# Buffers and due times of the weighed edge scores in a two-layer graph kernel: six for four, and eight held chunks for nine

## The chip, the cores and the metric

The kernel runs on one core of one Trainium2 chip. The metric is the device time of one execution in microseconds (us); lower is better. A profiled execution is one run with the hardware profiler on; its times are told from the start of its span.

## What is computed

The inputs are `x`, 16 batches of 1024 nodes with 256 features, one sparse 1024 x 1024 matrix `adj` that is used in both layers, and small weights, all in float32. The first layer is an attention over `adj`; the second scores every edge and sends messages along it. Cut to what matters:

```
# layer 0, for each batch
feats = x @ W1.T;  f1 = feats @ W2 + b2
h = softmax(leaky_relu(f1[:, None] + f1[None, :]) + adj) @ feats + bias2 + x
# layer 1, for each batch
hidden[u, v] = relu(h[u] @ W1u + h[v] @ W1v + b1)
S[u, v] = sigmoid(hidden[u, v] @ W2 + b2)
a[v] = sum_u S[u, v] * adj[u, v] * h[u]
m[v] = (sum_u adj[u, v] * h[u]) * h[v]
out = beta1 * h + beta2 * (a @ Wa + ba) + beta3 * (m @ Wm + bm)
```

S counts only where `adj` isn't zero, so it is worked out for listed edges alone.

## The kernel before, in words

**Groups and chunks.** The 16 batches are taken in three groups of 5, 5 and 6 (`GROUPS`; 0, 1 and 2 here). Nodes are cut into 8 chunks of 128. For each group the core writes the two ends of the edge scores (`pu_d`, `pw_d`), h times Wa (`ha_d`) and the rest of the output (`zb_d`) to HBM, scores the edges, and at last sums over edges.

**Scores.** The edge list has 135 slots of 128 edges each (`SLOTS`). For a slot and all batches of a group POOL gathers a row of each edge's end (`fetch`, L1212 for the u side and L1219 for the v side; five buffers `gv`), DVE compares it with the other end (`compare`, L1248), ACT sums it, one instruction a batch (`sums`, L1262; every eighth slot of group 2 on DVE, L1259), and after each part of 4 to 16 slots ACT applies tanh (`gates`, L1270) and DVE adds one (L1289). POOL scatters the scores of each slot into the dense SA of the group in HBM (`scatter`, L1228). The scatters stand in a list `late`, out of which one or two are taken at each slot and all that are left at the end.

**The sum over edges.** The groups come in the order 1, 0, 2. For each group, each of the 8 column chunks `vc` and each of the 8 row chunks `c` there is one chunk of work, 192 in all and numbered here from 0 in this order: SP loads the 128 x 128 scores of all the group's batches (`load_sa`, L1332, tile `sat`, `SA` = 7 buffers); ACT copies them apart by batch (`part_sa`, L1345, tile `apart`, four buffers); DVE multiplies them by `adj` (`weigh_sa`, L1350, in place); PE multiplies them with h times Wa (`gather`, L1363, one matmul for each batch, which the trace shows as two instructions of 256 columns). After the eighth row chunk DVE adds the sum to the rest of the output (`finish_z`, L1386), ACT's queue stores it (`store_z`, L1390), and SP's queue loads the rest of a later column chunk (`load_zb`, L1373, two buffers).

**Held chunks of h times Wa.** PE's other operand, `ha_g`, is held for all 8 row chunks of a group, 640 KB each, in a ring of `HA` = 9 buffers (`load_ha`, L1318). There are 24 loads, numbered by group order and row chunk. A load can leave when the chunk `HA` places before it was read for the last time, in the eighth column chunk of its group. The sixth batch of group 2 lies in another tile, `rest`.

**What sets the order.** Nothing is left to a scheduler. Each step is put into a `Timetable` (L347) with a due time, and all are emitted in the order of due times; each engine and each DMA queue works in that order. PE's due times come from a running sum of matmul columns (a chunk of groups 0 and 1 is 5 x 256 columns, 2.13 us; one of group 2 2.56 us), the others are set relative to it. `begins[p]` is when PE is due to begin chunk p. Copies stand 8.2 us and weighings 6.0 us ahead of it (L1720, L1721). A load of SA stands 4.0 us ahead of the chunk 7 places before, whose buffer it takes (L1716). The slots of a group are evenly spaced between two set times; in group 2 from 1351.3 to 1872.0 in the table, so 3.86 us apart. The loads of `ha_g` beyond the first nine stand 2.4 us after the begin of the chunk that frees their buffer (L1711, L1712); the ninth stands in group 1's second column chunk (L1709). Between the halves of most column chunks PE also works off messages of batches that were put off (`follows`), with no chunk of the edge sum in them; there is none inside or behind the last column chunk of group 0, and a long one stands between groups 1 and 0.

The program says of the buffers and due times:

```python
    HA = 9
    SA = 7
...
        apart = st["apart", g, vc, c] = room(g).tile(
            [P, SIZE[g], P], F32, name="apart", bufs=4
        )
...
        due = when[0] - 36.0 + 4.0 * i if i < SA else begins[parts[i - SA]] - 4.0
...
        times.at(begins[p] - 8.2, lambda p=p: part_sa(*p))
        times.at(begins[p] - 6.0, lambda p=p: weigh_sa(*p))
```

Of the kernel before, what the change touches and what calls it, by code (L numbers as in the profile page):

```python
# [8 lines left out]
F32 = mybir.dt.float32  # L9
# [5 lines left out]
P = 128  # L15
# [356 lines left out]
def edge_layers(  # L372
# [40 lines left out]
    NG = len(GROUPS)  # L413
    SIZE = [hi - lo for lo, hi in GROUPS]
# [786 lines left out]

    PARTS = [16, 32, 48, 64, 80, 96, 112, 124, 131, len(SLOTS)]
    AHEAD = GV - 2
    HA = 9
    SA = 7
    late = []

# [105 lines left out]
    def room(g):  # L1313
        return pools["last" if g + 1 == NG else "late"]

    def load_ha(g, c):
        st["ha", g, c] = pools["late"].tile([P, CUT * D], F32, name="ha_g", bufs=HA)
        nc.sync.dma_start(  # L1318
            out=st["ha", g, c], in_=ha_d[g][c * P : (c + 1) * P, : CUT * D]
        )  # L1320
# [7 lines left out]
    def load_sa(g, vc, c):  # L1328

        n = SIZE[g]  # L1330
        sat = st["sat", g, vc, c] = room(g).tile([P, P, n], F32, name="sat", bufs=SA)
        nc.sync.dma_start(  # L1332
            out=sat.rearrange("p v g -> p (v g)"),
            in_=sa_d[g].rearrange("(c p v) g -> c p (v g)", p=P, v=N)[
                c, :, vc * P * n : (vc + 1) * P * n
            ],
        )

    def part_sa(g, vc, c):

        sat = st.pop(("sat", g, vc, c))
        apart = st["apart", g, vc, c] = room(g).tile(
            [P, SIZE[g], P], F32, name="apart", bufs=4
        )
        nc.scalar.copy(apart.rearrange("p g v -> p v g"), sat)  # L1345

    def weigh_sa(g, vc, c):
        apart = st["apart", g, vc, c]
        a = adj_sb[:, c, vc * P : (vc + 1) * P]
        nc.vector.tensor_tensor(  # L1350
            apart, apart, a.unsqueeze(1).to_broadcast([P, SIZE[g], P]), ALU.mult
        )
# [108 lines left out]
    times = Timetable()  # L1461
# [196 lines left out]
    when = []  # L1658
    begins = {}
# [17 lines left out]
    due = when[last] - 30.0  # L1677
# [27 lines left out]
    for n, (g, c) in enumerate((g, c) for g in order for c in range(C)):  # L1705
        if n < C:
            due = opened + 2.0 + (when[0] - 14.0 - opened) * n / C
        elif n < HA:
            due = when[2 + n - C] + 0.1  # L1709
        else:  # L1710
            k, c1 = divmod(n - HA, C)  # L1711
            due = begins[order[k], C - 1, c1] + 2.4  # L1712
        times.at(due, lambda g=g, c=c: load_ha(g, c))
    parts = list(begins)
    for i, p in enumerate(parts):
        due = when[0] - 36.0 + 4.0 * i if i < SA else begins[parts[i - SA]] - 4.0  # L1716
        if p[0] + 1 == NG:
            due = max(due, ended + 0.1 + 0.01 * i)
        times.at(due, lambda p=p: load_sa(*p))
        times.at(begins[p] - 8.2, lambda p=p: part_sa(*p))  # L1720
        times.at(begins[p] - 6.0, lambda p=p: weigh_sa(*p))  # L1721
    for i, (g, vc, half) in enumerate(halves):
        if half == 0:
            due = when[0] - 20.0 + 8.0 * i if i < 4 else when[i - 2] + 5.0
            if g + 1 == NG:
                due = max(due, ended + 0.2)
# [4 lines left out]
@with_exitstack  # L1731
def tile_graph_layers(ctx: ExitStack, tc: tile.TileContext, *args):
    nc = tc.nc
    I32 = mybir.dt.int32
    hold = ctx.enter_context(tc.tile_pool(name="hold", bufs=1))
    flag = hold.tile([1, 1], I32, name="flag")
    edge_layers(tc, *args, flag)
    over = nc.values_load(
        flag[0:1, 0:1],
        min_val=0,  # L1740
        max_val=1,
        skip_runtime_bounds_check_because="it is a comparison's result",
    )
    with tc.If(over > 0):
        dense_layers(tc, *args)
# [43 lines left out]
```

## Time and profile before

| what | us |
| --- | --- |
| three timed runs | 2081.66, 2082.96, 2084.30 (median 2082.96) |
| the profiled execution, own time | 2087.25 |
| its span | 2085.5 |
| PE busy in the span | 2023.7 |
| DVE, ACT, POOL busy | 1569.9, 1374.0, 1137.4 |
| first matmul of the edge sum, of group 0, of group 2 | 1419.6, 1680.8, 1910.6 |
| last matmul of the edge sum starts | 2078.2 |

The mean granted clock of TensorE is 0.997 of full speed. A row of the page's groups has the line, the engine, the operation and its tiles (output, arrow, inputs), how often it ran, its busy time and mean length, and behind the second bar the idle time of the engine just before it and who ended that. A row of the waits has who waited, for whom, the us in total, the times and the longest. In the timeline a row has its start, its length, engine, line and tiles; "SPq" and "ACTq" are the issue of a DMA by that queue, and a DMA lands later than its row ends. Tiles are named as in the program: `sat` is SA as loaded, `apart` SA copied apart and weighed, `ha_g` h times Wa, `gv` the gathered ends, `lg` the scores, `sa_d` SA in HBM, `pzg` and `pzh` the outputs of the edge sum.

### The profile page before, as it was taken

How to read it: one execution, taken by the hardware profiler on the slowest of the kernel's cores; microseconds unless marked ns; L12 is line 12 of the kernel's file. 1: busy time of each engine (PE TensorE's matmuls, PEld its weight loads, DVE VectorE, ACT ScalarE, POOL GpSimd, SP SyncE). 2: the span in 40 equal slices, each digit the busy share in tenths (PEclk: the TensorE clock that was granted, in tenths of full speed). 3: DMA queues.
4: the chain of work that ended last, by engine and by line, in shares of the span. 5: the costliest groups of instructions: out<-in, count | busy, mean ns of one | idle time of the engine just before them, and what ended most of it. 6: DMA issues, size and time to landing. Idle time of an engine off the chain costs nothing.

```text
span 2085.5 us, 28967 instructions
## 1 busy us (share of the span) xinstructions
PE 2023.7 (97%) x8577; PEld 1551.1 (74%) x8577; DVE 1569.9 (75%) x2348; ACT 1374.0 (66%) x4842; POOL 1137.4 (55%) x974
## 2 busy tenths in 40 slices
PE   8999999999999999999999999899999989999998
PEld 6888887777776868677888886457676666768887
DVE  7799884677877777677878886578888878885544
ACT  4211222577777767687888777577888878886654
POOL 1122221267676767678777777666767766773000
PEclk9999999999999999999999999999999999999999
DMA  6689776788888889789999989899999999997773
GB/s 219 244 310 347 286 294 244 255 262 285 286 279 270 282 283 293 262 293 297 318 300 323 328 302 312 317 396 414 382 392 366 412 415 397 387 402 265 282 234 123
DMA packets 250007, 644.37 MB, mean 309 GB/s; under 512 B 38642, under 2 KB 139762, under 8 KB 247794
## 3 DMA queue, kind: packets, MB, share of 16 engines
q0 software_dynamic: 82016, 348.87, 47.7%
q1 hardware_dynamic: 132002, 259.36, 33.8%
q10 hardware_dynamic: 35824, 34.22, 4.7%
q8 instruction: 69, 1.13, 0.2%
q14 instruction: 96, 0.79, 0.1%
HBM read 479.56 MB, written 162.92 MB: 308 GB/s over the span
## 4 chain that ended last, share of the span: by engine, by line
PE 53%; DMA 18%; DVE 12%; ACT 8%; issue 6%; POOL 3%; SPq 0%; ACTq 0%; POOLq 0%; DVEq 0%
PE pv L1060 16%; DMA gv<-pw_d,idx_v 10%; PE pm L1158 9%; PE pp L1098 7%; PE pzg L1363 6%; DVE gv L1248 5%; PE pf L1006 4%; ACT gv L1262 4%; PE pea L1126 3%; DMA sat<-sa_d 3%; PE pzh L1363 3%; PE pz L1178 2%; ACT apart L1345 2%; DMA ha_g<-ha_d 2%; POOL sa_d L1228 2%
## 5 line engine op out<-in xcount | busy, mean ns | idle before, releaser
L1262 ACT ACTIVATE gv<-gv 128x272 f32<-128x272 f32 x2058 | 856.1, 419 | 308.2 <-DVE gv L1248 202.3
L1248 DVE TENSOR_TENSOR gv<-gv,gu 128x680 f32<-128x680 f32 (+1 forms) x810 | 706.5, 909 | 110.5 <-DMA gv<-pw_d,idx_v 106.1
L1219 POOL DMA_INDIRECT gv<-pw_d,idx_v x405 | 487.6, 1204 | 307.3 <-ACT gv L1262 197.0
L1228 POOL DMA_INDIRECT sa_d<-lg,idx_s x405 | 509.2, 1257 | 135.1 <-issue 109.5
L1060 PE MATMUL pv<-feats,eT 128*128 128x257 f32 x2048 | 468.9, 381 | 7.3 <-DVE eT L1047 6.7
L1158 PE MATMUL pm<-adj_sb,xh 128*128 128x512 f32 x1024 | 450.9, 593 | 1.7 <-DVE xh L1074 1.7
L1060 PEld LDWEIGHTS pv<-feats,eT 128*128 128x128 f32 x2048 | 381.1, 189 | 71.4 <-DVE eT L1047 14.9
L1262 ACT ACTIVATION_READ_ACCUMULATOR gv<-gv 128x1 f32 x2058 | 388.9, 189 | 0.0
L1363 PE MATMUL pzg<-ha_g,apart 128*128 128x256 f32 x1536 | 367.1, 382 | 22.2 <-DVE apart L1350 21.8
L1158 PEld LDWEIGHTS pm<-adj_sb,xh 128*128 128x128 f32 x1024 | 193.6, 191 | 220.2 <-issue 217.6
L1363 PEld LDWEIGHTS pzg<-ha_g,apart 128*128 128x128 f32 x1536 | 288.3, 190 | 83.6 <-DVE apart L1350 36.9
L1345 ACT COPY apart<-sat 128x640 f32<-128x640 f32 (+1 forms) x192 | 264.6, 1392 | 82.8 <-PE pzh L1363 38.7
L1350 DVE TENSOR_TENSOR apart<-apart,adj_sb 128x640 f32<-128x640 f32 (+1 forms) x192 | 166.3, 868 | 130.0 <-ACT apart L1345 129.4
L1098 PE MATMUL pp<-wuv,hT 128*128 128x272 f32 x1024 | 250.4, 394 | 6.7 <-ACT end L1112 3.8
L1098 PEld LDWEIGHTS pp<-wuv,hT 128*128 128x128 f32 x1024 | 194.6, 191 | 53.4 <-issue 6.2
L1047 DVE SCALAR_TENSOR_TENSOR eT<-row,col,grown 128x512 f32<-128x512 f32 x256 | 183.0, 746 | 24.6 <-ACT col L993 23.8
L852 POOL DMA_INDIRECT table_d<-rec,at x52 | 57.4, 1105 | 252.2 <-DVE rec L845 154.9
L1091 ACT COPY hT<-ph 128x512 f32<-128x512 f32 x96 | 55.2, 576 | 109.3 <-PE ph L1080 109.1
L1126 PE MATMUL pea<-wa,hT 128*128 128x256 f32 x512 | 121.4, 380 | 0.0
L1178 PE MATMUL pz<-wm,mT 128*128 128x256 f32 x512 | 116.0, 379 | 0.2 <-DVE mT L1169 0.2
L1006 PE MATMUL pf<-w1T,xT 128*128 128x257 f32 x512 | 114.1, 380 | 0.9 <-DVE xT L964 0.9
L1363 PE MATMUL pzh<-ha_g,apart 128*128 128x256 f32 x384 | 114.2, 379 | 0.0
(179 smaller groups left out, 1588.6 us busy)
## 6 DMA issues: line engine op xcount, KB each, us to landing
sa_d<-zero SPq DMA_DIRECT2D x128, 512.0 KB, 5.7
sat<-sa_d SPq DMA_DIRECT2D x128, 320.0 KB, 9.3
sat<-sa_d SPq DMA_DIRECT2D x64, 384.0 KB, 4.8
pu_d<-end SPq DMA_DIRECT2D x64, 272.0 KB, 4.9
pw_d<-end SPq DMA_DIRECT2D x64, 272.0 KB, 5.9
ha_d<-ea SPq DMA_DIRECT2D x64, 256.0 KB, 6.0
zb_d<-zb ACTq DMA_DIRECT2D x64, 256.0 KB, 6.8
xh<-in_x_dram SPq DMA_DIRECT2D x15, 1024.0 KB, 12.4
```

What stands on the lines that cost most here:

```text
L1006: nc.tensor.matmul(pfs[i], lhsT=st["xT"][:, h, c * P : (c + 1) * P], rhs=w1T[:, h, :], start=(h == 0), stop=(h == H - 1),)
L1047: nc.vector.scalar_tensor_tensor(st["eT", b, k, n][:, i, :], st["row"][:, cols], st["col"][:, j : j + 1], grown[:, j, cols], ALU.max, ALU. ...
L1060: nc.tensor.matmul(pv[:, : D + 1], lhsT=st["eT", b, k, j // 4][:, j % 4, i * P : (i + 1) * P], rhs=st["feats", b][:, j, :], start=(j == 0) ...
L1098: nc.tensor.matmul(pp[:, k, :R], lhsT=st["hTi", b, i][:, h, k * P : (k + 1) * P], rhs=wuv[:, side, h, :], start=(h == 0), stop=(h == H - 1),)
L1126: nc.tensor.matmul(pp[:, k, :], lhsT=st["hTi", b, i][:, h, k * P : (k + 1) * P], rhs=wa[:, h, :], start=(h == 0), stop=(h == H - 1),)
L1158: nc.tensor.matmul(pm, lhsT=held[b][:, c, h * P : (h + 1) * P], rhs=adj_sb[:, c, span], start=(c == 0), stop=(c == C - 1),)
L1219: nc.gpsimd.indirect_dma_start(out=gv, out_offset=None, in_=pw_d[g], in_offset=bass.IndirectOffsetOnAxis(ap=idx_v[:, t, s : s + 1], axis=0),)
L1228: dma = nc.gpsimd.indirect_dma_start(out=sa_d[g], out_offset=bass.IndirectOffsetOnAxis(ap=idx_s[:, t, s : s + 1], axis=0), in_=lg[:, i, : ...
L1248: nc.vector.tensor_tensor(mv, mv, mu, op)
L1262: nc.scalar.activation(one[:, j, :], one[:, j, :], AF.Copy, accum_out=lg[:, i, j : j + 1])
L1345: nc.scalar.copy(apart.rearrange("p g v -> p v g"), sat)
L1363: nc.tensor.matmul(st["pzg", g, vc][j // 4][:, j % 4, :], lhsT=apart[:, j, :], rhs=ha, start=(c == 0 and j % 2 == 0), stop=(c == C - 1 and ...
```

## The change

The ring of `apart` has six buffers for groups 0 and 1 and four, as before, for group 2. `HA` goes from 9 to 8. In bytes a partition, two buffers of 5 x 128 floats take what one of 5 x 256 floats gives. For chunks of groups 0 and 1 the copies, the weighings, and the loads of SA from the eighth on stand 3.6 us sooner in the timetable. With `HA` = 8 the middle branch of the `ha_g` due times (L1708) is never taken, so each load from the ninth on waits for the chunk eight places before it.

```diff
-    HA = 9
+    HA = 8
     SA = 7
...
-            [P, SIZE[g], P], F32, name="apart", bufs=4
+            [P, SIZE[g], P], F32, name="apart", bufs=4 if g + 1 == NG else 6
...
     for i, p in enumerate(parts):
-        due = when[0] - 36.0 + 4.0 * i if i < SA else begins[parts[i - SA]] - 4.0
+        sooner = 0.0 if p[0] + 1 == NG else 3.6
+        due = when[0] - 36.0 + 4.0 * i if i < SA else begins[parts[i - SA]] - 4.0 - sooner
         if p[0] + 1 == NG:
             due = max(due, ended + 0.1 + 0.01 * i)
         times.at(due, lambda p=p: load_sa(*p))
-        times.at(begins[p] - 8.2, lambda p=p: part_sa(*p))
-        times.at(begins[p] - 6.0, lambda p=p: weigh_sa(*p))
+        times.at(begins[p] - 8.2 - sooner, lambda p=p: part_sa(*p))
+        times.at(begins[p] - 6.0 - sooner, lambda p=p: weigh_sa(*p))
```

## The prediction

> **What bounds the kernel now.** I read the page first, then the waits of each engine by stage, then single chunks in the timeline. The page says that PE is nearly full:
>
> ```profile
> PE 2023.7 (97%) x8577; PEld 1551.1 (74%) x8577; DVE 1569.9 (75%) x2348; ACT 1374.0 (66%) x4842; POOL 1137.4 (55%) x974
> ...
> L1363 PE MATMUL pzg<-ha_g,apart 128*128 128x256 f32 x1536 | 367.1, 382 | 22.2 <-DVE apart L1350 21.8
> ```
>
> So only 62 us of the span are idle on PE, and 21.8 of them stand ahead of the matmuls that read the weighed SA, the tiles which this change buffers. The other edits can't win more than that. The waits of PE from 1419 to 1912, the stage of groups 1 and 0 (128 of the 192 chunks), put almost all of it there (the columns are us in total, times, longest):
>
> ```profile
> PE pzg L1363 <- DVE apart L1350: 20.8, 27, 1.8
> ```
>
> Who holds whom is told by ACT's waits from 1420 to 1888,
>
> ```profile
> ACT gv L1262 <- DVE gv L1248: 46.3, 25, 4.9
> ...
> ACT apart L1345 <- DMA sat<-sa_d: 3.9, 2, 2.0
> ```
>
> by ACT's from 1888 to 1912, and by SP's from 1888 to 1936:
>
> ```profile
> ACT apart L1345 <- PE pzh L1363: 4.6, 3, 3.0
> ```
>
> ```profile
> SPq L1332 <- DMA sa_d<-lg,idx_s: 13.0, 1, 13.0
> ```
>
> In the whole of 1420 to 1888 nothing but SP's queue waits for PE (1.6 us); ACT's 4.6 us on PE, the ring of four, all come after 1892. PE follows there. Against the timetable's own due times, the copy of chunk 4 ran 14.7 us early and that of chunk 116 12.6 us late, a slip of 27.3; the matmuls of the same chunks slipped 26.3, and the comparisons of score slots 26 and 132 slipped 28. Copies and scores slip together on ACT and DVE, and PE is towed.
>
> What they lose time to is read from the windows (busy us of PE, PEld, DVE, ACT, POOL, then clock, DMA share, GB/s):
>
> ```profile
> 1420.00:1880.00 460.00, 438.81 (x1717) 315.85 (x1716) 388.56 (x444) 390.65 (x1322) 324.99 (x240) 1.00 1.01 396
> 1880.00:1903.00 23.00, 23.00 (x105) 19.70 (x104) 14.53 (x19) 17.49 (x34) 17.22 (x15) 1.00 0.44 127
> 1903.00:1936.00 33.00, 32.00 (x145) 26.84 (x144) 14.74 (x15) 17.30 (x13) 0.00 (x0) 1.00 0.99 385
> ```
>
> The DMA engines are taken up to 1880, half empty while the last scatters trickle out, then full again. The timeline shows the gate between the second and the third line:
>
> ```profile
> 1900.53 0.97 POOL L1228 DMA_INDIRECT sa_d<-lg,idx_s  x1 [0.30 <-issue]
> ...
> 1902.93 0.80 SPq L1332 DMA_DIRECT2D sat<-sa_d  x2
> ...
> 1903.83 0.37 SPq L1318 DMA_DIRECT2D ha_g<-ha_d  x1
> ...
> 1906.73 2.89 ACT L1345 COPY apart<-sat 128x768 f32<-128x768 f32 x2 [3.28 <-DMA sat<-sa_d]
> ...
> 1908.28 0.96 DVE L1350 TENSOR_TENSOR apart<-apart,adj_sb 128x768 f32<-128x768 f32 x1 [3.97 <-ACT apart L1345]
> ...
> 1910.58 1.89 PE L1363 MATMUL pzg<-ha_g,apart 128*128 128x256 f32 x8
> ```
>
> Group 2's SA can't be loaded before group 2's last scatter has landed (1902.6); SP stood 13.0 us for that. Load, copy and weighing end at 1909.24, and PE arrives at 1910.58. So PE has **1.3 us** of slack at this gate, whatever it saves before. After it PE runs full to the end.
>
> **The change part by part.** The sum is against the profiled execution: span 2085.5, own time 2087.25, 1.75 us around it; that is 4.29 us above the median of the three runs, 2082.96, to which I carry the difference over unchanged.
>
> Copies and weighings 3.6 us sooner, six buffers. Nothing is added: 128 copies at 1.33 us and 128 weighings at 0.83 us keep their size (the medians). 3.6 us is 1.7 chunks of 2.13 us in the table, and the two more buffers give back 4.27, so ACT waits no more for a buffer than before. Each PE wait is at most 1.8 us, so most of the 20.8 are covered at first. But the tow isn't cut: copies and scores still slip 27 us, and PE can only be 3.6 us further ahead of them than now. It reaches the gate 3.6 us sooner at most, and waits there. Worth: the slack of 1.3 us, cut to **0.4** by the next item. If the tow were cut, it would be up to 20.8.
>
> The Trainium skill's Perfetto Trace Analysis, Optimization Strategy, says that a gap which repeats on the engine that should be full can mean too few buffers. Its rule would put 20.8 us here, a median of 2062.2 before the cost of the held chunks; here no row from 1420 to 1888 shows a wait for a buffer of this ring.
>
> Eight chunks of h times Wa. The same 24 loads of 640 KB are made, each from the ninth one load later in the ring. At the turn from group 1 to 0 this is hidden: eight loads leave at 1631 to 1672, the last lands at 1695.0, and the same slots now carry chunks 0 to 7, where 7 is read at 1701.5 (1698 if PE is 3.6 ahead), since 33 us of other matmuls stand between the groups (1648 to 1681). Without that cover the last would cost its 22.9 us of latency less seven chunks of 2.16, so 7.8. At the turn to group 2 there are no such matmuls. Chunk 0 was long there; now it takes the first slot behind SP's 13 us stand, and each chunk the slot of the next one. Slots leave at 1903.83, 1904.77, 1908.03, 1910.63, 1911.60, 1913.77, 1918.90; they landed at 1910.2, 1912.7, 1917.2, about 1920, 1923.0, 1926.2 and about 1929.5 (two are not recorded and set between their neighbours). A chunk takes 2.59 us on PE. So it starts at 1910.2 (0.4 early), 1912.8, 1917.2 (a wait of 1.8), 1920.0, 1923.0, 1926.2, 1929.5 and 1932.1, and the next column chunk at 1934.8 in place of 1933.2, since the eighth load, 655,360 bytes at the 407 GB/s of 1910 to 1920, puts the SA behind it off by 1.6 us. Cost with the 0.4 in it: **+1.6**. Ends: -0.4, if the loads land in time, and +3.4, if the last takes the 12.4 us of the slowest there and not 10.6. I take the walk, whose rows are this very place.
>
> The Trainium skill's DMA: Bandwidth & Descriptors, Where 436 GB/s comes from, states that loads from HBM are bound at about 358 GB/s for a core. By it the eighth load would be 1.83 us (an estimate from that page); the trace moved 410 to 421 GB/s in most 10 us stretches of this stage, so the measured rate decides.
>
> Loads of SA 3.6 us sooner. On SP they pass, once a column chunk, the load of z, behind which SP stood 119.1 us in 13 waits for output stores; one to two more loads leave ahead of each stand. Most lie landed for 10 to 20 us before they are copied, so it is worth nothing where that lead holds. It doesn't around 1701 to 1712, where ACT waited 2.0 and 1.9 us for SA that took 16 us to land.
>
> The gate itself. One load of 640 KB (that at 1445) leaves the full stage: at most -1.6 us. The weighing of chunk 115 now stands ahead of the comparison of slot 131, whose end lets POOL fetch the last row at 1870.97 and then put out 20 scatters back to back: +0.8. Nothing is moved on POOL's queue. Ends: -3.7 (those 1.6 and the one wait of 2.1 us of a copy behind the z sum, which it may now pass) and +3.6 (ACT held for the whole of the move); I take 0, as the two priced rows nearly cancel.
>
> Sum: +1.6 us. 2087.25 becomes 2088.9, and the median 2082.96 becomes **2084.6**.
>
> **The rivals.**
> - The tow is cut (faster). Copies and scores may slip because they wait for one another in one unlucky order: DVE waits 45.1 us for copies, ACT 46.3 for comparisons. If the score stream gains what PE does, the gate moves too: 2082.96 - 20.8 + 1.6 = 2063.8, or half of it, 2074. Against: the distance from copy to weighing stays 2.2 us, and 3.6 us is nearly one score slot of 3.86, so the order among them hardly changes; DMA is full. Chance 0.18.
> - ACT is held by SA that has not landed (slower). A copy 3.6 us sooner in ACT's list waits where the load is bound by the DMA engines, and the sums behind it wait too, then POOL's fetches, the last scatter, the gate. Price 3.6 us in a jam; two jams are in sight (1416 to 1437, landing 10.4 to 20.7 us, and 1681 to 1714). With +1.6 that is 2088.2, with both 2091.8. It decides from 2.6 us of such hold that reaches the last scatter. For: the 3.9 us ACT waits there already. Against: the loads are sooner too. Chance 0.30, and 0.05 for a costlier turn to group 2.
> - The change doesn't do what it says: the PE waits stay, since the weighings wait for copies whose SA is late. As the gate doesn't move, the time is the same 2084.6; it is within the forecast.
>
> **How the numbers follow.** Forecast, gate unmoved: 0.47, its own range 2079 to 2087. 0.2% is 4.2 us, about what a measurement of this kernel can tell from no change: within it 0.47, faster 0.18, slower 0.35. The range takes in the ends (-0.4 - 3.7 and +3.4 + 3.6, so 2078.9 to 2090.0), both jams nearly, and the faster rival down to where half the tow is cut: 2075 to 2091. Outside lie about 0.1 on each side.
>
> **What would show it.** Right: PE's waits for the weighings fall from 20.8 us to under 8 in groups 1 and 0, a new wait of 2 to 4 us stands at the first chunks of group 2, first for SA, then for h times Wa, and the last scatter still lands at 1902 to 1904. The tow cut: the last scatter lands before 1898. ACT held: its waits for SA grow from 3.9 us, and the last scatter lands after 1905. What would make it wrong most of all is the gate: each us by which the last scatter moves is a us of the result.

## The result and the profile after

The changed kernel took **2094.43 us** (median of 11 runs, 2090.39 to 2096.82); the kernel before took 2084.30 beside it on the same chip (11 runs, 2079.47 to 2090.87). The ratio is 1.0041, with a 95% interval of 1.0030 to 1.0052: slower by 0.4%. The two medians lie 10.1 us apart, and the ratio makes some 8.5 us. The forecast was 2084.6 in a range of 2075 to 2091, so the time lies outside it, on the slower side. The profiled execution after has an own time of 2096.5 us and a span of 2094.8, 9.3 us more than before.

The page after, its rows of busy time and of the two groups that the change touches:

```profile
PE 2029.3 (97%) x8577; PEld 1554.2 (74%) x8577; DVE 1568.3 (75%) x2348; ACT 1372.4 (66%) x4842; POOL 1126.5 (54%) x974
...
L1363 PE MATMUL pzg<-ha_g,apart 128*128 128x256 f32 x1536 | 367.3, 382 | 19.7 <-DVE apart L1350 14.9
...
L1345 ACT COPY apart<-sat 128x640 f32<-128x640 f32 (+1 forms) x192 | 264.5, 1390 | 78.6 <-PE pzh L1363 33.7
```

DVE, ACT and POOL work no longer than before. PE's 5.6 us more are about what its granted clock makes (0.994 of full speed, 0.997 before: 0.3% of 2029 is 6). PE's idle time ahead of these matmuls fell from 22.2 to 19.7 us, and yet the span grew. PE's longest waits in the stage of groups 1 and 0 (from 1419 to 1912), and those at the start of group 2 (from 1915 to 1950; us in total, times, longest):

```profile
PE pzg L1363 <- DVE apart L1350: 14.9, 20, 1.8
PE pm L1158 <- DVE zb L1188: 3.0, 3, 1.3
PE ph L1080 <- DVE zb L1188: 1.5, 1, 1.5
```

```profile
PE pzg L1363 <- DMA ha_g<-ha_d: 4.4, 4, 2.6
```

The waits for weighings went from 20.8 to 14.9, but PE now waits for DVE in the matmuls of the rest of the output (L1158, L1080) as well, and in group 2 for h times Wa. ACT's waits from 1420 to 1888, and SP's from 1888 to 1945:

```profile
ACT gv L1262 <- DVE gv L1248: 53.9, 22, 6.3
...
ACT gv L1262 <- DMA sat<-sa_d: 8.2, 1, 8.2
```

```profile
SPq L1332 <- DMA sa_d<-lg,idx_s: 14.7, 1, 14.7
```

The row of 8.2 us is the one to look at: a **sum of scores** on ACT (`sums`, L1262) waits for a load of SA, which it doesn't read. The gate, in the timeline after:

```profile
1907.62 0.97 POOL L1228 DMA_INDIRECT sa_d<-lg,idx_s  x1 [0.31 <-issue]
...
1909.99 0.80 SPq L1332 DMA_DIRECT2D sat<-sa_d  x2
...
1913.44 2.84 ACT L1345 COPY apart<-sat 128x768 f32<-128x768 f32 x2 [7.88 <-DMA sat<-sa_d]
...
1917.52 2.53 PE L1363 MATMUL pzg<-ha_g,apart 128*128 128x256 f32 x8 [2.65 <-DMA ha_g<-ha_d]
```

The last scatter leaves at 1907.6 in place of 1900.5, and what stands behind it is about as much later.

**Where the 9.3 us are.** Three stretches, read from the first starts of these instructions in both traces, add up to it: the first matmul of group 1 is 1.7 us later (it varied from 1417.6 to 1422.3 among the four kernels e9 to e12 of this study on one chip, so I don't explain it); from there to the last scatter 486.3 us in place of 480.9 (+5.4); from the last scatter to the thirteenth chunk of group 2 45.3 in place of 43.2 (+2.2). From there to the end of the last matmul both take 134.8. The thirteenth chunk of group 2 is the fifth row chunk of its second column chunk. The expectations below call this point the second column chunk; that itself begins some 10.4 us sooner, 22.7 us behind the first matmul of group 2 before and 25.1 after, so the difference is nearly the same.

The 5.4 arise in one place. The comparison of score slot 24 starts 14.7 us after the first matmul of group 1 in place of 9.4, and from slot 24 to slot 132 the kernels take 444.8 and 445.0. So the score stream is set back by 5.3 us in one place, and keeps that to the gate. The place, in ACT's timeline before:

```profile
1406.84 1.30 ACT L1345 COPY apart<-sat 128x640 f32<-128x640 f32 x1
...
1412.33 0.37 ACTq L1194 DMA_DIRECT2D zb_d<-zb  x1
1412.74 0.43 ACT L1262 ACTIVATE gv<-gv 128x272 f32<-128x272 f32 x1 [1.20 <-DMA zb_d<-zb]
...
1418.85 0.37 ACTq L1194 DMA_DIRECT2D zb_d<-zb  x1
1419.26 0.43 ACT L1262 ACTIVATE gv<-gv 128x272 f32<-128x272 f32 x1 [4.05 <-DMA sat<-sa_d]
```

and after:

```profile
1408.56 3.61 ACT L1345 COPY apart<-sat 128x640 f32<-128x640 f32 x3
...
1421.31 0.37 ACTq L1194 DMA_DIRECT2D zb_d<-zb  x1
1421.73 0.43 ACT L1262 ACTIVATE gv<-gv 128x272 f32<-128x272 f32 x1 [8.18 <-DMA sat<-sa_d]
```

"ACTq L1194" is ACT issuing a store of `zb`, the rest of the output (`store_product`); in brackets is how long the next instruction waited and for what. Before, one copy stands ahead of the first store; after, three do, and the store leaves 9 us later. ACT stands for it 8.2 us with everything behind it. POOL then stands longer still, since it can't fetch into a buffer `gv` that ACT hasn't summed:

```profile
1416.82 1.02 POOL L1228 DMA_INDIRECT sa_d<-lg,idx_s  x1 [0.30 <-issue]
1429.05 0.95 POOL L1219 DMA_INDIRECT gv<-pw_d,idx_v  x1 [11.21 <-ACT gv L1262]
```

The setback shows as time in which ACT stands, not as more work put in front of the sums. In the 27 us from 12 us ahead of the first matmul of group 1 to 15 us behind it ACT is busy 19.3 us before and 14.3 after, so it stands 5.0 us more, and it begins 7 copies before and 6 after (columns as in the windows of the prediction):

```profile
1407.58:1434.58 27.00, 27.00 (x107) 20.02 (x106) 20.25 (x25) 19.28 (x64) 15.99 (x14) 1.00 1.02 415
1409.30:1436.30 27.00, 26.68 (x104) 19.26 (x103) 15.50 (x20) 14.31 (x45) 11.33 (x11) 1.00 1.02 408
```

What does the store wait for? In the trace each DMA that SP and ACT issue carries one of eight numbers, 100 to 107, which go round: each names a counter that tells of the DMA's landing. The store of 1421.31 has the number that the load of SA issued at 1401.54 had, whose issue looks so:

```profile
L1332 SPq DMA_DIRECT2D sat<-sa_d x1: 320/320/320, 1401.5 to 1401.5; - x1
...
  ACT gv L1262: 8.2, 1
...
DMA to landing us min/median/max: 19.7/19.7/19.7
```

It landed at 1421.24, and the store left 0.07 us later. The store before, of 1412.33, shared its number with an older store of `zb`, which landed at 1412.25. That is the first reading; the experiments test it.

### The profile page after: what moved, and what is told of

Same layout as the page of the kernel before. It is cut to its first block, busy times and chain, and to the rows that moved or that the text cites. A ratio compares the mean times of both kernels' runs of the same rounds, so it can differ in the third digit from the quotient of the medians.

```text
span 2094.8 us, 28917 instructions
## 1 busy us (share of the span) xinstructions
PE 2029.3 (97%) x8577; PEld 1554.2 (74%) x8577; DVE 1568.3 (75%) x2348; ACT 1372.4 (66%) x4842; POOL 1126.5 (54%) x974
## 3 DMA queue, kind: packets, MB, share of 16 engines
q1 hardware_dynamic: 132002, 259.36, 33.8%
## 5 line engine op out<-in xcount | busy, mean ns | idle before, releaser
L1262 ACT ACTIVATE gv<-gv 128x272 f32<-128x272 f32 x2058 | 856.1, 419 | 323.4 <-DVE gv L1248 207.4
L1228 POOL DMA_INDIRECT sa_d<-lg,idx_s x405 | 497.6, 1229 | 137.6 <-issue 107.5
L1158 PE MATMUL pm<-adj_sb,xh 128*128 128x512 f32 x1024 | 454.2, 597 | 7.1 <-DVE zb L1188 3.0
L1060 PEld LDWEIGHTS pv<-feats,eT 128*128 128x128 f32 x2048 | 381.4, 190 | 70.6 <-DVE eT L1047 14.9
L1262 ACT ACTIVATION_READ_ACCUMULATOR gv<-gv 128x1 f32 x2058 | 389.2, 189 | 0.0
L1363 PE MATMUL pzg<-ha_g,apart 128*128 128x256 f32 x1536 | 367.3, 382 | 19.7 <-DVE apart L1350 14.9
L1158 PEld LDWEIGHTS pm<-adj_sb,xh 128*128 128x128 f32 x1024 | 194.6, 191 | 228.4 <-issue 220.0
L1345 ACT COPY apart<-sat 128x640 f32<-128x640 f32 (+1 forms) x192 | 264.5, 1390 | 78.6 <-PE pzh L1363 33.7
```

Source lines behind the costliest of these rows:

```text
L1060: nc.tensor.matmul(pv[:, : D + 1], lhsT=st["eT", b, k, j // 4][:, j % 4, i * P : (i + 1) * P], rhs=st["feats", b][:, j, :], start=(j == 0) ...
L1158: nc.tensor.matmul(pm, lhsT=held[b][:, c, h * P : (h + 1) * P], rhs=adj_sb[:, c, span], start=(c == 0), stop=(c == C - 1),)
L1228: dma = nc.gpsimd.indirect_dma_start(out=sa_d[g], out_offset=bass.IndirectOffsetOnAxis(ap=idx_s[:, t, s : s + 1], axis=0), in_=lg[:, i, : ...
L1262: nc.scalar.activation(one[:, j, :], one[:, j, :], AF.Copy, accum_out=lg[:, i, j : j + 1])
L1363: nc.tensor.matmul(st["pzg", g, vc][j // 4][:, j % 4, :], lhsT=apart[:, j, :], rhs=ha, start=(c == 0 and j % 2 == 0), stop=(c == C - 1 and ...
```

## The experiments

Each ratio is against runs of the kernel before on the same chip, taken beside it: its median there was 2108.73 (e1 to e4), 2116.97 (e5 to e8), 2084.89 (e9 to e12), 2085.28 (e13 to e16) and 2108.31 (e17, e18). Of each trace I give four stretches. **Slot 24**: from the first matmul of group 1 to the comparison of that slot (9.4 before, 14.7 after). **Stage**: from the same matmul to the first of group 2 (491.0, 496.2). **To the gate**: from it to the last scatter (480.9, 486.3). **Start of group 2**: from its first matmul to its thirteenth chunk (33.1, 35.4). On the chip of e1 to e4 the first matmul of group 1 starts 13 to 27 us later than in the two profiles above, so the absolute times in their expectations can't be held against their traces, and the stretches are compared.

The first theories: A, loads of SA moved ahead hold the store of zb on ACT, and the eighth held chunk costs 2.3 us; rival B, the order of copies and weighings on ACT and DVE sets the scores back; rival C, the eighth chunk costs all of it.

**e1: eight held chunks alone**, in the kernel before.

```diff
-    HA = 9
+    HA = 8
```

> The kernel before with eight held chunks in place of nine and nothing else. Theory A (ACT's first store of zb near 1420 waits for the landing of a load of SA which now stands ahead of it, the score stream and the gate of group 2 slip 6 to 7 us; the held chunk costs 2.3 us more behind the gate): ACT's wait near 1420 stays at 4 us, the last scatter lands at 1901 to 1905, PE waits 2 to 4 us for h times Wa at group 2, time 1.0005 to 1.002 of before. Rival B (the order of copies and weighings on ACT and DVE costs the gate): the same as A here. Rival C (the eighth held chunk costs all of it): the last scatter lands after 1907, 1.003 to 1.005.

Measured: 2109.31, ratio 1.0004 (0.9986 to 1.0021). Slot 24 at 9.7, start of group 2 35.4. C falls; 2.3 us show in the trace, and the interval of 0.17% either way is too wide for them.

**e2: the changed kernel with the loads of SA at their old due times.**

```diff
-        due = when[0] - 36.0 + 4.0 * i if i < SA else begins[parts[i - SA]] - 4.0 - sooner
+        due = when[0] - 36.0 + 4.0 * i if i < SA else begins[parts[i - SA]] - 4.0
```

> The kernel after with the loads of SA at their old due times; copies and weighings stay 3.6 us sooner, six buffers, eight held chunks. Theory A: ACT's wait near 1420 returns from 8.2 us to about 4, the last scatter lands at 1902 to 1905, 1.001 to 1.002 of before. Rival B: the wait may fall but the last scatter still lands after 1907, 1.003 to 1.005. Rival C: no change from after, 1.003 to 1.005.

Measured: 2116.50, ratio 1.0041 (1.0023 to 1.0060). Slot 24 at 13.2, stage 496.6: all of the loss, without the sooner loads.

**e3: the kernel before with the loads alone 3.6 us sooner.**

```diff
-        due = when[0] - 36.0 + 4.0 * i if i < SA else begins[parts[i - SA]] - 4.0
+        due = when[0] - 36.0 + 4.0 * i if i < SA else begins[parts[i - SA]] - 4.0 - (0.0 if p[0] + 1 == NG else 3.6)
```

> The kernel before with the loads of SA alone 3.6 us sooner; four buffers, nine held chunks, copies and weighings as before. Theory A: ACT's wait near 1420 rises to about 8 us, the last scatter lands after 1906, 1.002 to 1.004 of before. Rivals B and C: the last scatter lands at 1901 to 1904, 0.999 to 1.001.

Measured: 2106.74, ratio 0.9994 (0.9976 to 1.0013). Slot 24 at 8.1, stage 486.3. With e2 this fells theory A: the loads cost nothing, the copies bring the stand.

**e4: the changed kernel with the first four loads of h times Wa of group 2 ahead of its first SA on SP.**

```diff
+            if g + 1 == NG and c < 4:
+                due = min(due, begins[order[k], C - 1, 1] - 4.1 + 0.01 * c)
```

> The kernel after with the first four loads of h times Wa of group 2 put ahead of the first load of group 2's SA in SP's order, so that they leave while SP would stand for the last scatter. All theories: the last scatter stays where it is in after (1907 to 1911). Theory A: PE's waits for h times Wa at group 2 (4.4 us) go below 1 us and 2 to 3.5 us of the time come back, 1.002 to 1.003 of before. Rival C: most of it comes back, 1.000 to 1.001.

Measured: 2117.55, ratio 1.0051 (1.0029 to 1.0073). The start of group 2 falls to 32.8, but it begins later: 12.5 us after the last scatter against 9.9 in the changed kernel. The edit moved the wait and took none away; A (1.002 to 1.003) and C (1.000 to 1.001) both miss.

Theory A2 from here on: the copies, standing ahead of the first stores of zb, make ACT stand there. B2: they cost a little at every chunk.

**e5: the changed kernel, the first eight chunks at their old due times.**

```diff
-        sooner = 0.0 if p[0] + 1 == NG else 3.6
+        sooner = 0.0 if p[0] + 1 == NG or i < C else 3.6
```

> The changed kernel, but the first eight chunks of SA (the first column chunk of group 1) are loaded, copied and weighed at their old due times; all later chunks of groups 1 and 0 stay 3.6 us sooner, ring of six and eight held chunks stay. In the runs so far the stage from the first matmul of group 1 to the first of group 2 took 486 to 491 us with the copies at their old times and 496 to 497 us with the copies sooner, and the score stream fell back by 4 to 6 us against the first matmul within its first 25 slots (14.7, 13.2 and 13.9 us from the first matmul to the comparison of slot 24, against 9.4, 9.7 and 8.1). Theory A2: the loss is one event at the start of the stage: ScalarE has done its copies early, issues the first store of zb sooner in the order of DMAs, and stands there 7 to 8 us behind a load of SA. With the first eight chunks at their old times the event is gone: ScalarE's longest stand between 1405 and 1440 (times as in the profile before) falls to 5 us or less, slot 24 comes 8 to 10.5 us after the first matmul, the stage takes 486 to 491 us, and the ratio to the kernel before is 1.000 to 1.002 (the eighth held chunk alone is left). Rival B2: the copies and weighings sooner cost a little at every chunk; then 120 of 128 chunks still pay: the stage takes 495 us or more, the ratio is 1.003 to 1.005.

Measured: 2122.15, ratio 1.0020 (0.9999 to 1.0040). Slot 24 at 10.1, stage 488.7, so the setback is gone though 120 of 128 chunks are still sooner. The ratio lies at the edge of what A2 allowed, and its interval doesn't keep out B2's 1.003; the stage does, 488.7 where B2 had 495 or more. ACT's timeline there has the old order again, with no stand at either store:

```profile
1439.50 1.31 ACT L1345 COPY apart<-sat 128x640 f32<-128x640 f32 x1
...
1445.99 0.37 ACTq L1194 DMA_DIRECT2D zb_d<-zb  x1
1446.41 0.43 ACT L1262 ACTIVATE gv<-gv 128x272 f32<-128x272 f32 x1 [0.81 <-DVE zb L1188]
1446.84 1.32 ACT L1345 COPY apart<-sat 128x640 f32<-128x640 f32 x1
1448.63 0.37 ACTq L1194 DMA_DIRECT2D zb_d<-zb  x1
1449.04 0.43 ACT L1262 ACTIVATE gv<-gv 128x272 f32<-128x272 f32 x1 [0.16 <-issue]
```

**e6: the kernel before, the copies and weighings of four chunks (of 192) sooner.**

```diff
-        times.at(begins[p] - 8.2, lambda p=p: part_sa(*p))
-        times.at(begins[p] - 6.0, lambda p=p: weigh_sa(*p))
+        sooner = 3.6 if i < 4 else 0.0
+        times.at(begins[p] - 8.2 - sooner, lambda p=p: part_sa(*p))
+        times.at(begins[p] - 6.0 - sooner, lambda p=p: weigh_sa(*p))
```

> The kernel before with one edit: the copies and weighings of the first four chunks of SA (of 192) come 3.6 us sooner; ring of four, nine held chunks, loads as before. One look, so the stage is read from the trace. Theory A2: these four chunks alone bring the whole event: ScalarE stands 7 us or more near the first store of zb, slot 24 comes 13 to 15 us after the first matmul of group 1, and the stage to the first matmul of group 2 takes 494 to 497 us against 491 before. Rival B2 (a little at every chunk): no event; slot 24 at 8 to 10 us and the stage at 487 to 491 us.

One run, 2127.13. Slot 24 at 13.7: four chunks bring the whole setback of that slot. The last scatter leaves 482.6 us after the first matmul, so at the gate less of it is seen than in the changed kernel (486.3). ACT's timeline is that of the changed kernel over again:

```profile
1445.14 3.61 ACT L1345 COPY apart<-sat 128x640 f32<-128x640 f32 x3
...
1457.62 0.37 ACTq L1194 DMA_DIRECT2D zb_d<-zb  x1
1458.04 0.43 ACT L1262 ACTIVATE gv<-gv 128x272 f32<-128x272 f32 x1 [7.89 <-DMA sat<-sa_d]
```

The stage is 492.0, less than the 494 to 497 expected; a single trace of an unmoved stage lies between 486.3 and 491.3 in this study, so this length alone settles nothing.

**e7 and e8: the stores of zb issued by SP**, in the changed kernel and in the kernel before.

```diff
-        nc.scalar.dma_start(
+        nc.sync.dma_start(
             out=zb_d[g][2 * i * P : (2 * i + 2) * P, j * D : (j + 1) * D].rearrange(
```

> The changed kernel with one edit: the stores of zb are issued by SyncE in place of ScalarE, at the same due times. Theory A2: ScalarE no longer stands at a store; its longest idle stretch between 1405 and 1440 is 5 us or less, slot 24 comes 8 to 10.5 us after the first matmul of group 1, the stage to the first matmul of group 2 takes 486 to 491 us, ratio to the kernel before 0.998 to 1.002. What can spoil it: SyncE now stands where ScalarE stood, and the loads of SA behind the store come as much later. Rival B2: who issues the store doesn't matter, the stage stays at 495 us or more, ratio 1.003 to 1.005.

> The kernel before with the same one edit: the stores of zb are issued by SyncE in place of ScalarE. Theory A2: the kernel before pays a small form of the same stand (1.2 and 4.1 us for ScalarE near 1420), so it gains 0 to 4 us: ratio 0.998 to 1.000, slot 24 at 8 us or less after the first matmul. Rival B2: the same as before, 1.000, slot 24 at 9 to 10 us.

Measured: e7 2124.77, ratio 1.0022 (1.0003 to 1.0041), slot 24 at 11.5, stage 493.0; e8 2123.02, ratio 1.0029 (1.0003 to 1.0055), slot 24 at 10.0, stage 489.0. Both miss. In e7 ACT is free of the store, but the landing holds DVE instead, in its waits from 1443 to 1461:

```profile
DVE zb L1188 <- DMA zb_d<-zb: 5.6, 1, 5.6
```

`zb` has two buffers; the product of the third waits until the first is stored, and the comparisons stand behind it on DVE. Why e8 lost time stays open: its trace shows 1.7 us more than the kernel before from the last scatter to the thirteenth chunk of group 2, not the 6 us of the ratio's middle.

The Trainium skill, DMA: Bandwidth & Descriptors, section Issuing engines are not separate DMA queues, says that it saves only the sequencer's time to issue from several engines, and calls that time small beside the transfer. Here the issue itself took 0.37 us and the store landed 7.9 us after it, which agrees; the stand ahead of the issue took 8.2 us, so what the store costs ACT is not the issue.

**e9: the changed kernel with both turns at old due times and the edit of e4.** Theory A3 adds a second event of the kind at the turn from group 1 to 0.

```diff
-        sooner = 0.0 if p[0] + 1 == NG else 3.6
+        sooner = 0.0 if p[0] + 1 == NG or i < C or 7 * C <= i < 9 * C else 3.6
```

> The changed kernel with its three suspected costs taken out together: the chunks at the start of group 1 (the first eight) and around the turn to group 0 (the last eight of group 1, the first eight of group 0) keep their old due times, and the first four chunks of h times Wa of group 2 are loaded ahead of its first SA. 104 of 128 chunks are still loaded, copied and weighed 3.6 us sooner, with the ring of six and eight held chunks. Theory A3 (two events, at the two places where ScalarE issues stores of zb among the early copies, and the late chunk of h times Wa): stage from the first matmul of group 1 to the first of group 2 486 to 491 us, slot 24 at 8 to 10.5 us, 33 us from there to the second column chunk of group 2, ratio to the kernel before 0.999 to 1.0015. Rival B2 (a little at every chunk): the stage 494 us or more, ratio 1.002 to 1.004.

Measured: 2089.50, ratio 1.0023 (1.0014 to 1.0032). Slot 24 at 8.7, start of group 2 33.8, but the ratio is above what A3 allowed. SP's timeline shows the fault of the loads that were put ahead:

```profile
1891.51 4.64 SPq L1318 DMA_DIRECT2D ha_g<-ha_d  x3
1902.78 1.75 SPq L1332 DMA_DIRECT2D sat<-sa_d  x4
```

The last scatter left at 1896.3, and the first SA 6.5 us later (2.4 before). So the edit saves nothing: from the last scatter to the thirteenth chunk of group 2 it takes 46.3 us here and 45.3 in e4, against 45.3 in the changed kernel. That leaves 3.3 us over the kernel before with nine chunks, 0.16%, at the lower part of the interval; what else e9 lost its profile doesn't show.

**e10: the changed kernel once more**, on this chip.

> The changed kernel once more, unaltered, beside the mended one on the same chip. All theories: ratio to the kernel before 1.003 to 1.005; slot 24 at 13 to 15 us after the first matmul of group 1, the stage to group 2 at 495 to 497 us, 35.5 us from there to the second column chunk.

Measured: 2093.94, ratio 1.0041 (1.0025 to 1.0057). Slot 24 at 14.0, stands of 7.8 and 3.7 us at the two stores, start of group 2 36.1. The stage was 490.8, 4 us under what was expected; against e11 and e12, which ran beside it, it is 2.5 to 3.3 more.

**e11: the kernel before, the twelve chunks around the turn to group 0 sooner** (`60 <= i < 72` in the edit of e6).

> The kernel before, with the copies and weighings of twelve chunks around the turn from group 1 to group 0 (the last four of group 1, the first eight of group 0) 3.6 us sooner; ring of four, nine held chunks, loads as before. One look, read from the trace. Theory A3: slot 24 stays at 8 to 10.5 us, but ScalarE stands 3 to 7 us within the turn, and slot 90 comes 107 to 109 us after slot 64 against 105.5; a part or all of it may be made up by slot 98 (140.9 before, 139.8 in the changed kernel). If there is no second event: slot 90 at 105 to 106 us.

One run, 2084.20. Slot 90 comes 106.8 us after slot 64, against 105.4 before, between what the two sides expected, and slot 98 after 140.7, against 140.9. ACT's longest wait for a DMA from 1655 to 1725 is 2.2 us, not the 3 to 7 of A3. So no second event is shown. Slot 24 comes at 10.9, above the 8 to 10.5 expected, though no copy ahead of it was moved: a single trace strays by that much.

**e12: the ring of six and eight held chunks, every due time old.**

```diff
-    HA = 9
+    HA = 8
...
-            [P, SIZE[g], P], F32, name="apart", bufs=4
+            [P, SIZE[g], P], F32, name="apart", bufs=4 if g + 1 == NG else 6
```

> The kernel before with the ring of six for groups 1 and 0 and eight held chunks, but every load, copy and weighing at its old due time. One look, read from the trace. Theory A3: two buffers more, unused by any earlier copy, change nothing in groups 1 and 0: slot 24 at 8 to 10.5 us, the stage 486 to 491 us, and the eighth held chunk shows as 35.5 us from the first matmul of group 2 to its second column chunk, against 33.1 before. Rival (the ring itself costs, by where its buffers lie or by copies that start as soon as a buffer is free): the stage 494 us or more.

One run, 2085.03. Slot 24 at 8.8, stage 488.3, start of group 2 34.8: the ring itself costs nothing that this trace shows.

**e13: the changed kernel, the stores of zb 1.9 us sooner in the timetable**, so that the first stands behind two copies, not three. **e14: the same in the kernel before.**

```diff
-            times.at(time + 2.3, lambda i=i: store_product(b, i))
+            times.at(time + 0.4, lambda i=i: store_product(b, i))
```

> The changed kernel with one edit: the stores of zb are put 0.4 us in place of 2.3 us behind their product, so that they stand one copy earlier in ScalarE's order; at the start of group 1 the first two then take the DMA counters whose last users are the load of h times Wa issued at 1398.5 and the load of z at 1405.4, in place of the two loads of SA issued at 1401.5 and 1408.7 (times of the changed kernel's trace). Copies and weighings stay 3.6 us sooner. Theory A4 (ScalarE stands for the landing of the DMA that last used the store's counter): the first store is issued near 1415 to 1416 in place of 1421.3, the longest stand of ScalarE there is 3 to 5 us in place of 7.8 to 8.2, slot 24 comes 9.5 to 12 us after the first matmul of group 1 (13.9 and 14.7 in the changed kernel), ratio to the kernel before 1.001 to 1.003. Rival B2 (the copies' order itself): slot 24 stays at 13.5 to 15, ratio 1.0035 to 1.005.

> The kernel before with the same edit alone. There the first store of group 1 keeps its counter and the second takes the one before. Theory A4: little to gain, ScalarE's stands of 1.2 and 4.1 us shrink by 0 to 3 us: ratio 0.998 to 1.000, slot 24 at 7 to 10 us. Rival B2: 1.000.

Measured: e13 2093.90, ratio 1.0038 (1.0025 to 1.0051), slot 24 at 13.2; e14 2087.86, ratio 1.0010 (0.9998 to 1.0022), slot 24 at 9.6. ACT's timeline of e13:

```profile
1409.88 2.45 ACT L1345 COPY apart<-sat 128x640 f32<-128x640 f32 x2
1419.39 0.37 ACTq L1194 DMA_DIRECT2D zb_d<-zb  x1
1419.80 1.31 ACT L1345 COPY apart<-sat 128x640 f32<-128x640 f32 x1 [7.47 <-DMA ha_g<-ha_d]
...
1424.93 0.37 ACTq L1194 DMA_DIRECT2D zb_d<-zb  x1
1425.34 0.43 ACT L1262 ACTIVATE gv<-gv 128x272 f32<-128x272 f32 x1 [3.51 <-DMA zg<-zb_d]
```

The kind of the stand is as A4 said and its size is not. So the stand didn't shrink, slot 24 lies between what A4 and B2 expected, the ratio is B2's, and e13 doesn't decide between the two. ACT now waits for a load of h times Wa and a load of z, which the store has nothing to do with; they landed at 1419.31 and 1424.85, and the stores left 0.08 us behind each. I had expected the load of h times Wa by 1416; it took 19.8 us to land. So the numbers decide whom ACT waits for, and here each choice was equally slow.

The same reading of seven traces (number of each store, who had it last, ACT's stand in us):

| run | first store | second store | both stands |
| --- | --- | --- | --- |
| before | 107, a store of zb | 101, SA | 1.2 + 4.1 |
| e5 | 106, h | 100, h times Wa | 0.8 + 0.0 |
| e15 | 106, h | 100, h times Wa | 2.3 + 0.8 |
| after | 101, SA | 103, SA | 8.2 + 4.1 |
| e6 | 101, SA | 103, SA | 7.9 + 3.6 |
| e10 | 101, SA | 103, SA | 7.8 + 3.7 |
| e13 | 100, h times Wa | 102, z | 7.5 + 3.5 |

In these and all other runs in which ACT issues the two stores, the last user was issued 16.3 to 20.7 us ahead of the store. Of these runs, those with three or two copies ahead of the first store stand 10.8 to 12.2 us at the two, those with one 0.8 to 8.1.

**e15: the changed kernel with both turns at old due times and no other edit** (the diff of e9). **e16: the kernel of e12, timed.**

> The changed kernel with the old due times for the first eight chunks of group 1 and the sixteen around the turn to group 0; the other 104 chunks stay sooner; no other edit. Theory A4: only the eighth held chunk is left, 2 to 2.5 us from the last scatter to the second column chunk of group 2: ratio 1.0005 to 1.0015, slot 24 at 8 to 10.5 us, last scatter 477 to 480 us after the first matmul of group 1. If the sooner copies of the other 104 chunks cost something too: 1.002 or more.

> The kernel of the look before (ring of six, eight held chunks, every due time old), timed. All theories but one: the eighth held chunk alone, 2 to 2.5 us: ratio 1.0005 to 1.0015. If the held chunk is hidden in the time: 0.999 to 1.0005.

Measured: e15 2087.30, ratio 1.0008 (0.9999 to 1.0017), slot 24 at 7.3, 480.3 to the gate; e16 2086.65, ratio 1.0012 (1.0000 to 1.0025). The two are alike, so the 104 chunks that are sooner in e15 neither cost nor gain more than the intervals leave room for, some 3 us either way (an estimate from the two). Two things in e15's trace miss: slot 24 comes below the 8 to 10.5 expected, and from the last scatter to the thirteenth chunk of group 2 it takes 3.8 us more than the kernel before, not 2 to 2.5. The sooner chunks do cut PE's waits as the change meant, to 14.1 us where e16, which has the six buffers but copies at the old times, has 18.7; from the first matmul of group 1 to that of group 2 in e15:

```profile
PE pzg L1363 <- DVE apart L1350: 14.1, 19, 1.5
```

The Trainium skill's Perfetto Trace Analysis, Optimization Strategy, says that gaps which repeat on the engine that should be full can come from too few buffers. e15 has the two buffers more, uses them, has 14.1 us of these gaps where 20.8 were, and is not faster; so here the measurement doesn't bear that reading out.

**e17: the kernel of e5 again. e18: the kernel of e11, timed.**

> The changed kernel with the old due times for the first eight chunks alone, once more. If the start of group 1 holds nearly all of the turns' cost: ratio 1.0005 to 1.002, as with both turns old. If the turn to group 0 holds half of it: 1.002 to 1.003.

> The kernel before with the copies and weighings of the twelve chunks around the turn to group 0 sooner, timed. If the start of group 1 holds nearly all: 0.9995 to 1.0007, since what the turn loses by slot 90 it makes up by slot 98. If this turn holds half: 1.001 to 1.002.

Measured: e17 2112.38, ratio 1.0016 (1.0001 to 1.0030); e18 2110.29, ratio 1.0005 (0.9988 to 1.0022). Both are what was expected if the start of group 1 holds nearly all, though each interval still reaches into what was expected if the turn to group 0 held half.

**All traces together.** The 7 with the first copies early (after, e2, e4, e6, e7, e10, e13) reach slot 24 13.4 us after the first matmul of group 1 on average and the gate after 484.2; the 13 others after 9.2 and 479.3. The sets don't overlap: slot 24 comes at 11.5 to 14.7 in the first and at 7.3 to 10.9 in the second, and the shortest way to the gate of the first set, 482.1, is longer than the longest of the second, 481.1. So the first copies, moved ahead, cost **5.0 us** at the gate. In the 27 us around the first matmul of group 1 that are shown above for two traces, ACT stands 11.0 to 12.7 us in the six early ones in which it issues the stores, 9.3 in e7, and 5.0 to 9.2 in the 13 others, and it begins 5 to 7 copies in all of them: slot 24 is late where ACT stands, and not where more copies stand ahead of the sums. From the last scatter to the thirteenth chunk of group 2, the kernels with nine held chunks (e8 aside, whose stores are on SP) take 43.0 on average, those with eight (without the edit of e4) 45.3: **2.3 us**. Together 7.3, or 0.35%, where 0.41% was measured (0.30 to 0.52).

## Why the prediction was wrong, step by step

- **PE is towed.** Right. The weighings came sooner, PE's waits for them fell (to 14.9, not to under 8 as foretold), and no gain of PE shows in the time: e15, in which this part works undisturbed, is no faster than e16, which lacks it, within some 3 us. No tow was cut; the faster rival falls.
- **Eight held chunks: +1.6.** Right in kind. The wait of PE at the first chunks of group 2 stands there (2.6 us at the first of them, where the walk had 1.8 at the third), and the stretch from the last scatter to the thirteenth chunk is 2.3 us longer on average. The term was mis-sized by 0.7. One thing there the walk didn't have: behind its wait of 2.6 us PE's granted clock was 0.54 from 1919.0 to 1922.5, and the first chunk took 4.0 us in place of 2.59. That isn't the cost, though: the seven other kernels with eight chunks whose clock stayed at 1.00 in this stretch take 45.1 on average.
- **The loads of SA sooner are worth nothing.** Right: 0.9994 alone (e3), and the loss is whole without them (e2).
- **The gate itself: "I take 0".** This is the step that failed. Its end of +3.6 was named for ACT held for the whole of the move, and two rows that nearly cancel were taken as a reason for the middle (-1.6 and +0.8, which even so leave -0.8). The last scatter left 7.1 us later in the profiled execution, 5.4 of it behind the first matmul of group 1, and by the average of the traces 5.0. The prediction had looked at the queues of SP and POOL, and not at what stands on ACT between the copies: two DMA issues. The copies were moved past them, and ACT stood 8.2 us at the first.
- **The rival "ACT is held".** Nearest of all: ACT is held, in the jam at 1416 to 1437 that it named, the last scatter is past 1905, and its 2091.8 for two jams lies within the spread of the runs (2090.39 to 2096.82). But its mechanism was another, so that its number lies nearer is in part luck. It had the copies wait for their own SA, and its sign was to be ACT's waits for SA at L1345 growing from 3.9; they fell to 1.0. The copies ran without a wait, three in a row; the store behind them waited, and the sums behind that. The one jam cost more than the 3.6 of the move, because a stand doesn't end with the move: it ends with a landing, up to 20 us after the issue.
- **Readings that were off.** The share of 410 to 421 GB/s stood in 23 of the 46 stretches of 10 us from 1420 to 1880, which is half and not most, and SP's waits for PE in 1420 to 1888 add up to 1.4 us, not 1.6. Neither moves the sum.
- **What is not shown.** No run kept the copies early and freed ACT, DVE and POOL of the stand at once; e7 came nearest (slot 24 at 11.5, below the 13.2 to 14.7 of the six other early ones). So that the stand makes all of the setback is argued, from e5, e6, e15 and e17, where both come and go together, and from ACT's standing time in all traces; the size of the two stands isn't one to one with the setback (e14 stands 8.1 us in all and isn't set back). Why the first stores get another number when copies are moved past them wasn't traced (after and e10, the same program, have the same numbers). A third buffer of zb, which might have parted the two, wasn't tried.

## What to carry to other kernels

Before a step is moved on an engine, list what it is moved past, and look above all for DMA issues: ahead of the change ask what such an issue will wait for, and what stands behind it. A wait by an instruction for a tile that it doesn't read is the sign of it. And where the bound stream waits a little everywhere but is towed by another, buffers for it can win nothing, as here; count the gain at the place where the two streams meet.

## What the runs showed of the hardware

- The DMAs that SP and ACT issue in this kernel share eight numbers in turn, and an issue waits until the last DMA of its number has landed, whatever it carried. In the 20 traces 3268 issues have a last DMA of their number whose landing is recorded, and none left before it. Where such a wait ended last and the landing is recorded, ACT's stores left 0.07 or 0.08 us behind it (landing 1412.25, store 1412.33; 1421.24 and 1421.31; in e13 1419.31 and 1419.39, 1424.85 and 1424.93), and a load of SP 0.02 (1401.53 and 1401.54). So a store on ACT can stand for a load on SP.
- While the DMA engines were full (from 1400 to 1440 a share of 1.02 and 414 GB/s before, 1.01 and 396 after), the seven loads of 320 to 640 KB issued from 1396 to 1417 in these two traces whose landing is recorded took 17.1 to 21.4 us, against medians of 9.3 before and 8.4 after for those of 320 KB over the whole run. It is this time that one of eight numbers is taken for.
- The kernel before took 2084.3 to 2085.3 us on three chips and 2108.3 to 2117.0 on three others, with a median granted clock of 0.995 on two of the former and 0.993 on the latter. Most of it lies ahead of this change: the first matmul of group 1 starts at 1417.6 to 1422.3 on the former and at 1433.9 to 1460.7 on the latter. By what, the runs don't tell; 0.2% of clock is too little for 1.1 to 1.5% of time.
- In the five traces in which PE stood 2.6 to 4.4 us just ahead of the first matmul of group 2 (after, e4, e7, e9, e17), the granted clock of the 4.5 us from that matmul on is 0.50 to 0.64. In the 15 others, in which PE stood 0 to 1.2 us there, it is 1.00.
